# Layer 2 context attention: where the queries' reciprocal roots stand in VectorE's row

## The chip, the core and the metric

The kernel runs on one core of one Trainium2 chip. It is one launch of a program written in Python with a tiling layer: the source emits instructions in an order, and a planner of that layer (it has a cost for each instruction and a list of free buffers) decides the order in which each engine gets them. The engines are PE (TensorE: matrix products and transposes, writes to PSUM), DVE (VectorE), ACT (ScalarE), POOL (GpSimd, no access to PSUM) and SP (issues DMAs). Each runs its own row of instructions in order and waits on semaphores for the others. The metric is the device time of one execution in microseconds, the median of several runs; lower is better.

## What is computed

A decoder of four layers on x of 8 batches x 256 tokens x 256 features, with 77 context rows in each batch. Every layer has an attention, a context attention and a feed-forward part, each followed by a layer norm. The part in question is the context attention of layer 2. Its reference, cut:

```python
q = (x @ q_w.T + q_b).reshape(b, s1, H, hd).transpose(0, 2, 1, 3)      # H = 16, hd = 16
kv = (y @ kv_w.T + kv_b).reshape(b, s2, 2, H, hd).transpose(2, 0, 3, 1, 4)
k, v = (kv[0], kv[1])
q = _layernorm(q, qn_w, qn_b)          # over the 16 numbers of a head, eps 1e-6
k = _layernorm(k, kn_w, kn_b)
q = _apply_rope(q) * scale
attn = jax.nn.softmax(jnp.einsum('bhqd,bhkd->bhqk', q, k), axis=-1)
o = jnp.einsum('bhqk,bhkd->bhqd', attn, v)
return o.transpose(0, 2, 1, 3).reshape(b, s1, c) @ out_w.T + out_b
```

The feed-forward part behind it is a mixture of 14 experts. For every token it needs the two best experts and its place in their lists; this is called the routing here, and the kernel works it out batch by batch inside the context attention, as soon as a batch's layer norm is done.

## The kernel before, in words

A batch is 256 tokens, two tiles of 128. The function of the stage, `l2_xattn`, has one iteration for each of the 8 batches, and works on three of them at once: the weights of batch b, the scores' shift of batch b + 1, and the queries of batch b + 2.

- `queries(b)` projects values and queries on PE (L155). The query weights are centred beforehand, so the layer norm needs only the deviation: ACT squares the projection, DVE sums each head's 16 squares (L1630), and `roots` makes 1/sqrt of 32 numbers per token by integer arithmetic on DVE: scale (L1614), shift (L1615), seed (L1616) and three Newton rounds of three small operations (L1618, L1619, L1620), each of which needs the one before. Then the product of projection and root, 128 x 512, gives `q` (L1732). The projection stays in its PSUM buffer until then.
- `rotated(b, q, v)` does the rotation: two POOL instructions (L1743, in the trace `u`), two on DVE (L1747 and L1748, in the trace `sq`), and a POOL sum (L1749) into `qpad`. All their operands are in SBUF.
- `shift(b, qp, between)` transposes the queries (L293; copied by L141 on DVE and L143 on ACT), computes all scores once (L1763: for each of two tiles four PSUM buffers), and takes the negated maxima over the keys on DVE (L1767, eight of them, `mxp`). Then it calls `between`, and after that transposes the maxima (L1774) and adds them to the queries as one more coordinate (L1775).
- `weights` computes the scores transposed (L1786) and their exponentials on ACT (L1791). `weigh` is what `between` calls: the product with the values (L1805, 32 passes in two halves), copied to SBUF by ACT (L1811, first half) and DVE (L1807, second half). The copy on DVE waits by an explicit dependency for the end of the routing's first part.
- `heads_out` and `project` finish the batch: transposes (L1354), division (L1358, L1363), output projection (L155), residual (L272), layer norm (L249 to L255, with a root by POOL, L183) and transposes of the new x (L235).

Between these, `tick` advances a list of generators by one step each time it is called. For a batch that has its layer norm, `Routing.batch` is in that list. Its first part: product with the router's weights (PE, L155 `rw`), row maximum (DVE L2516), subtraction (L2517), exponential (ACT L2518), sum (L2519), reciprocal (L2520), product (L2521), the eight largest (MAX8, L2524), their indices (L2525), then small operations on them (L2568, L2526, L2570, L2532) up to `rsel`, the one-hot sum of the two chosen experts (L2535), and running counts (L2538). Its second part begins with PE products of `rsel` (L155 `upper`, `onesb`) for the places in the lists, and ends with four indirect DMAs by POOL (L1018).

PSUM has eight buffers of one tag, `ps`; a matrix product into a buffer waits until its former content has been read.

The loop, and where the order comes from:

```python
for b in range(NB):
    e, v = weights(b, q2), ahead[0][1]
    ahead.pop(0)
    if b + 2 < NB:
        begun = queries(b + 2)
    if b + 1 < NB:
        q2 = shift(b + 1, ahead[0][0], lambda: weigh(b, e, v))
    else:
        weigh(b, e, v)
    if b + 2 < NB:
        ahead.append(rotated(b + 2, *begun))
    self.tick()
```

So the root and the product of batch b + 2 are emitted ahead of the score maxima of batch b + 1. The planner interleaves: in the order that it builds, the first round and one operation of the second stand ahead of the first maximum, one Newton operation stands between each two of the next maxima, and the product L1732 between the sixth and the seventh.

## Time and profile before

| what | value |
|---|---|
| median of 3 runs | 3623.32 us (3618.66 to 3629.59) |
| time of the profiled execution | 3594.94 us |
| its span, first to last instruction | 3593.2 us |
| mean granted PE clock in it | 0.896 |
| busy in the span: PE, DVE, ACT, POOL | 86%, 51%, 29%, 26% |
| one batch of the stage, at 2633 us | 27.36 us: PE 22.29, DVE 19.45, ACT 7.22, POOL 11.19 busy |
| the stage in the trace | about 2515 to 2745 us |

How to read the lines below: a line of the timeline gives the start in us, the duration, the engine, the line of the source, the operation, the tile that is written and those that are read, their shapes, and how often; in brackets stands how long the engine was idle before it and what ended that. A line of the waits gives who waited for whom, us in total, how many times, and the longest. A line of the table by stretches gives the stretch, its length, busy time (and instructions) of PE, PE's weight loads, DVE, ACT and POOL, the granted clock of PE, the share of DMA and GB/s.

### The profile page before, as it was taken

How to read it: one execution, taken by the hardware profiler on the slowest of the kernel's cores; microseconds unless marked ns; L12 is line 12 of the kernel's file. 1: busy time of each engine (PE TensorE's matmuls, PEld its weight loads, DVE VectorE, ACT ScalarE, POOL GpSimd, SP SyncE). 2: the span in 40 equal slices, each digit the busy share in tenths (PEclk: the TensorE clock that was granted, in tenths of full speed). 3: DMA queues.
4: the chain of work that ended last, by engine and by line, in shares of the span. 5: the costliest groups of instructions: out<-in, count | busy, mean ns of one | idle time of the engine just before them, and what ended most of it. 6: DMA issues, size and time to landing. Idle time of an engine off the chain costs nothing. (4 is left out here: it accounts for less than half of the span.)

```text
span 3593.2 us, 49384 instructions
## 1 busy us (share of the span) xinstructions
PE 3102.3 (86%) x19146; PEld 2184.7 (61%) x19146; DVE 1834.9 (51%) x4823; ACT 1043.6 (29%) x2343; POOL 928.1 (26%) x1398
## 2 busy tenths in 40 slices
PE   4777589979997998998999999898787997778789
PEld 3444257658875665666555777565555785566556
DVE  7888546631116555776211221566675344677652
ACT  4666322212222332332111111344222111343311
POOL 2222513243314101222000000411343444312351
PEclk6777689979998999988999999999777998888889
DMA  9900100035541000001010333200002552000000
GB/s 338 305 2 1 48 7 19 19 108 181 179 144 47 1 25 25 13 14 60 15 36 0 119 124 119 62 1 8 7 19 83 198 196 77 22 1 7 12 5 19
DMA packets 132127, 239.47 MB, mean 67 GB/s; under 512 B 14568, under 2 KB 103920, under 8 KB 124208
## 3 DMA queue, kind: packets, MB, share of 16 engines
q1 hardware_dynamic: 107632, 136.25, 11.3%
q0 software_dynamic: 23104, 98.95, 7.9%
q8 instruction: 154, 2.52, 0.3%
q10 hardware_dynamic: 1152, 1.05, 0.1%
q14 instruction: 85, 0.70, 0.1%
HBM read 156.52 MB, written 79.69 MB: 66 GB/s over the span
## 5 line engine op out<-in xcount | busy, mean ns | idle before, releaser
L155 PE MATMUL ps<-xt,w 128*128 128x256 f32 (+1 forms) x1408 | 452.9, 472 | 3.3 <-issue 2.9
L155 PE MATMUL ps<-w,hT 128*128 128x256 f32 (+1 forms) x1792 | 397.4, 379 | 0.0
L155 PEld LDWEIGHTS ps<-w,hT 128*128 128x128 f32 (+1 forms) x1792 | 329.9, 186 | 56.5 <-issue 6.0
L155 PE MATMUL ps<-gT,w 128*128 128x256 f32 (+1 forms) x1472 | 357.4, 401 | 5.7 <-ACT gT L143 3.0
L155 PEld LDWEIGHTS ps<-xt,w 128*128 128x128 f32 x1408 | 268.7, 198 | 149.4 <-issue 125.0
L155 PEld LDWEIGHTS ps<-gT,w 128*128 128x128 f32 x1472 | 276.5, 191 | 76.8 <-ACT gT L143 3.9
L155 PE MATMUL ps<-w,oT 128*128 128x256 f32 x768 | 181.9, 390 | 3.3 <-DVE mv L251 1.8
L267 POOL TENSOR_TENSOR xb<-x,rows 128x256 f32<-128x256 f32 x96 | 71.6, 752 | 401.7 <-DVE res L272 393.7
L155 PEld LDWEIGHTS ps<-w,oT 128*128 128x128 f32 x768 | 146.4, 194 | 38.5 <-issue 14.1
L235 PE MATMUL ps<-ident,x 128*128 128x128 f32 x320 | 62.0, 307 | 79.5 <-DVE x L255 59.4
L1115 ACT ACTIVATE hT<-ps,more 128x256 f32<-128x256 f32 x152 | 71.9, 474 | 196.1 <-PE ps L155 196.1
L255 DVE TENSOR_SCALAR x<-res,mv,rs 128x256 f32<-128x256 f32 x128 | 57.4, 449 | 126.9 <-POOL rs L183 126.9
L1126 DVE COPY y<-ps 128x512 f32<-128x512 f32 x41 | 28.3, 690 | 174.7 <-PE ps L155 174.7
L1184 DVE TENSOR_TENSOR hT<-hT,ps 128x512 f32<-128x512 f32 x56 | 38.5, 688 | 154.2 <-PE ps L155 152.7
L677 ACT ACTIVATE e<-ps,nm 128x128 bf16<-128x128 f32 (+1 forms) x256 | 103.9, 458 | 40.1 <-DVE nm L672 24.1
L932 PE MATMUL ps<-ident,P 128*77 128x128 f32 x512 | 90.0, 303 | 25.5 <-POOL P L923 15.7
L1666 POOL TENSOR_TENSOR kpad<-kpad,rows 128x256 f32<-128x256 f32 (+1 forms) x10 | 7.3, 729 | 404.2 <-DVE hu L1615 316.9
L923 POOL TENSOR_TENSOR P<-P,z 128x1232 f32<-128x1232 f32 x24 | 54.1, 2252 | 219.6 <-DVE z L921 214.3
L183 POOL TENSOR_TENSOR rs<-rs,mhalf 128x1 f32<-128x1 f32 x192 | 106.1, 554 | 14.2
L932 PEld LDWEIGHTS ps<-ident,P 128*77 128x77 f32 x512 | 60.7, 157 | 73.4 <-issue 25.5
L947 PE MATMUL ps<-PT,V 77*64 77x256 f32 x512 | 98.5, 446 | 7.5 <-DVE PT L141 4.9
L1180 ACT ACTIVATE hT<-ps 128x512 f32<-128x512 f32 x56 | 33.4, 597 | 237.5 <-PE ps L155 237.5
(655 smaller groups left out, 6319.2 us busy)
## 6 DMA issues: line engine op xcount, KB each, us to landing
l2x<-zero SPq DMA_DIRECT2D x28, 1024.0 KB, 11.3
l0x<-zero SPq DMA_DIRECT2D x16, 1024.0 KB, 11.3
w<-in_L_ffn_rg SPq DMA_DIRECT2D x8, 1024.0 KB, 7.0
w<-in_L_ffn_ru SPq DMA_DIRECT2D x8, 1024.0 KB, 5.0
w<-in_L_ffn_rd SPq DMA_DIRECT2D x8, 1024.0 KB, 5.7
l2e<-y SPq DMA_DIRECT2D x22, 256.0 KB, 2.3
rows<-in_rows SPq DMA_DIRECT2D x9, 544.0 KB, 3.7
l0e<-y SPq DMA_DIRECT2D x19, 256.0 KB, 2.9
```

The lines of the kernel that those rows point to most:

```text
L155: self.nc.tensor.matmul(out, lhsT, rhs, start=(i == 0), stop=(i == last))
L183: self.nc.gpsimd.tensor_tensor(out, out, self.mhalf[: in_.shape[0], :w], ALU.pow)
L235: self.nc.tensor.transpose(ps[:, k * P : (k + 1) * P], x[:, k * P : (k + 1) * P], self.ident)
L255: nc.vector.tensor_scalar(t, r, mv[:, 0:1], rs, ALU.subtract, ALU.mult)
L267: self.nc.gpsimd.tensor_tensor(t, self.X[i], row, ALU.add)
L677: nc.scalar.activation(e[:, : (t + 1) * P], ps[j][:, i, :], AF.Exp, bias=nm[:, t, h : h + 1], accum_out=z[:, t, h : h + 1],)
L923: eng.tensor_tensor(pr, pr, z.unsqueeze(2).to_broadcast([P, H, SC]), ALU.mult)
L932: nc.tensor.transpose(psv[:, m, t * P : (t + 1) * P], Pt[t][:, 2 * n + m, :], self.ident)
L947: nc.tensor.matmul(po[64 * m : 64 * m + 64, :S], V[:, h * 64 : (h + 1) * 64], ahead[n % 2][:, m, :], start=True, stop=True,)
L1115: nc.scalar.activation(hT[:, f + m, :], ps[:, m * 256 : (m + 1) * 256], func, bias=more[:, f + m : f + m + 1])
L1180: nc.scalar.activation(hT[:, f, :], ps, func, **({"bias": bias(f)} if bias else {}))
L1184: nc.vector.tensor_tensor(hT[:, f, :], hT[:, f, :], ps, ALU.mult)
```

## The change

`deviations` now ends with the sum of squares and leaves the root to its callers; for the keys (`l2_keys`) the two calls follow each other as before. `queries` becomes a generator: its first step emits the projections, squares and sums, its second step the root and the product. The first two batches run both steps at once. In the loop the first step is taken where `queries` stood, and the second in `between`, that is, after all eight maxima and after the call of `tick` that emits the routing's first part, and ahead of `weigh`. `rotated` is emitted where it was.

```diff
@@ deviations
         nc.vector.tensor_reduce(v, sq, AX.X, ALU.add)
-        return self.roots(v, 1.0 / 16, 1e-6)
+        return v
@@ l2_keys
-                r = self.deviations(pool, kh, H)
+                r = self.roots(self.deviations(pool, kh, H), 1.0 / 16, 1e-6)
@@ queries
                 r = self.deviations(w2, ps.rearrange("p (n d) -> p n d", d=16), 32)
+                yield
+                r = self.roots(r, 1.0 / 16, 1e-6)
                 q = self.t(w2, [P, 2, H, 16], "q")
                 ...
-                return q, v
+                self.begun = q, v
@@ l2_xattn
+            def all_of(gen):
+                for _ in gen:
+                    pass
+                return self.begun
+
+            def between(b, e, v, gen):
+                all_of(gen)
+                weigh(b, e, v)
+
-            ahead = [rotated(0, *queries(0))]
-            begun = queries(1)
+            ahead = [rotated(0, *all_of(queries(0)))]
+            begun = all_of(queries(1))
...
-                if b + 2 < NB:
-                    begun = queries(b + 2)
+                gen = queries(b + 2) if b + 2 < NB else iter(())
+                next(gen, None)
                 if b + 1 < NB:
-                    q2 = shift(b + 1, ahead[0][0], lambda: weigh(b, e, v))
+                    q2 = shift(b + 1, ahead[0][0], lambda: between(b, e, v, gen))
...
-                    ahead.append(rotated(b + 2, *begun))
+                    ahead.append(rotated(b + 2, *self.begun))
```

Lines behind L1730 have other numbers in the changed kernel: the product L1732 is L1734 there, L1747 to L1749 are L1749 to L1751, the maxima L1767 are L1769, L1805 is L1807, and those of the routing are 11 higher (L2519 is L2530, `rsel` L2546).

## The prediction

> **What bounds the kernel now.** The page first: PE is busy 86% of the span, DVE 51%, but that is an average over twelve layers. The change touches only the L2 context attention, which stands in the trace from about 2515 to 2745 us. So I went to the waits inside the five batches that carry routing work (2570 to 2700 us; total us, times, longest):

> ```profile
> PE ps L155 <- DVE rsel L2535: 12.2, 5, 2.8
> ...
> PE ps L1763 <- DVE mxp L1767: 5.8, 5, 1.2
> ...
> DVE rm L2519 <- ACT rs L2518: 0.6, 1, 0.6
> ```

> TensorE stands still once in every batch for `rsel`, the routing's one-hot sum, which is the last of a long row of DVE instructions. All that PE does after it in the batch (routing ranks, transposes of the maxima, L1786 scores) is queued behind it, so the DVE row from the score maxima to `rsel` sets the batch. The timeline of the batch at 2605 us shows that row (start, us, engine, line):

> ```profile
> 2605.13 0.19 DVE L1618 TENSOR_TENSOR hu<-hy 128x32 f32<-128x32 f32 x1
> 2605.24 0.47 DVE L1767 TENSOR_REDUCE mxp<-ps 128x4 f32<-128x308 f32 x1
> ...
> 2607.95 3.64 PE L1805 MATMUL ps<-e,vp 77*32 77x256 f32 x32
> 2608.06 0.68 DVE L1732 TENSOR_TENSOR q<-ps,hy 128x512 f32<-128x512 f32 x1
> ...
> 2608.82 2.13 POOL L1743 TENSOR_TENSOR u<-q,other 128x256 f32<-128x256 f32 x2 [6.96 <-DVE q L1732]
> ...
> 2609.52 0.70 DVE L1747 TENSOR_TENSOR sq<-q,own 128x512 f32<-128x512 f32 x1
> ...
> 2609.94 0.59 ACT L1811 COPY oT<-ps 128x512 f32<-128x512 f32 x1 [7.92 <-PE ps L1805]
> ...
> 2610.14 0.17 DVE L2517 TENSOR_TENSOR rs<-ps,rm 128x28 f32<-128x28 f32 x1
> 2610.26 1.24 DVE L1748 TENSOR_TENSOR sq<-sq,more 128x512 f32<-128x512 f32 x1
> 2610.43 0.23 ACT L2518 ACTIVATE rs<-rs 128x28 f32<-128x28 f32 x1
> ...
> 2611.42 0.17 DVE L2519 TENSOR_REDUCE rm<-rs 128x2 f32<-128x28 f32 x1
> ...
> 2611.67 1.26 POOL L1749 TENSOR_TENSOR qpad<-sq,u 128x512 f32<-128x512 f32 x1 [0.72 <-PE ps L1805]
> 2611.82 1.15 DVE L2521 TENSOR_TENSOR rs<-rs,rm 128x28 f32<-128x28 f32 x1
> 2613.01 0.25 DVE L2524 MAX8 rv<-rs 128x8 f32<-128x14 f32 x2
> ...
> 2614.16 0.19 DVE L2535 TENSOR_TENSOR rsel<-rhot 128x28 bf16<-128x28 f32 x1
> ...
> 2614.40 0.19 PE L155 MATMUL ps<-rsel,upper 128*128 128x14 bf16 x1 [2.81 <-DVE rsel L2535]
> ```

> Three things are to be seen. DVE has no gap in this row. ACT's exponential (L2518) stands in ACT's queue behind the copy L1811, which waits for half of PE's L1805. And two DVE instructions are longer than their kind: L2521 takes 1.15 us here and 0.19 where POOL is idle (2718.93 us); L1748 takes 1.24 and 0.64 alone (2563.31 us). Each ends just after a POOL instruction does: DVE operations with two operands in SBUF wait for POOL's. The batches at 2633, 2660 and 2687 us repeat this to 0.2 us; batch lengths are 27.42, 27.36 and 27.35 us.

> **What the built order says.** No instruction is added or removed on any engine; PE, ACT, POOL and SP keep their order, no DMA moves, no PE instruction waits for the later query product. Only DVE's order changes, in six batches (queries 2 to 7). The planner does not put all the root behind the maxima: scale, shift, seed and the first Newton round stay ahead. After that: 4 maxima, round two (3 operations), 4 maxima, L2516, one operation, L2517, two operations, **L2519, product L1732**, L2520, L1747, L2521, L1748, MAX8. Before, round two and three and the product stood between the maxima.

> **Cost, in us after 2605.13** (before → after).
> - A copy now stands ahead of the scale instead of behind it, where it hid the scale's result: the copy's step 0.33 (2603.70 to 2604.03) plus scale to shift 0.21 (2555.13 to 2555.34), against 0.42: +0.12. The first maximum no longer waits for an operation of round two (a dependent step is 0.225): 0.11 → 0.01. PE's last scores wait for that maximum, so PE gains 0.10.
> - Maxima follow each other in 0.41 (eight in 3.34 at 2712.33: (3.34 − 0.47)/7). Round two, uncovered, is at 1.65, 1.87, 2.10; the second four start at 2.20, the last at 3.43 (before 3.91). L2516: 4.30 → 3.84; L2517: 5.01 → 4.05. Root operations end by 4.56.
> - **The new wait.** DVE now stands at L2519. The exponential was at 5.30 because of ACT's copy and PE's L1805; PE's 0.10 makes it 5.20, and its result is read 0.26 later (2584.25 to 2584.51): L2519 6.29 → 5.46, after 0.9 us of idle DVE. Queued behind it: the product and all of the rotation.
> - Product 2.93 → 5.55, ends 6.23. L1747 can start at 6.27, POOL's pair L1743 at 6.31 (0.08 behind the product, as now). Before, POOL's pair began at 3.69, beside maxima that read PSUM; now it meets L1747, L2521 and L1748, all with two SBUF operands. L1747 holds POOL to 6.88 (0.61, as at 2609.52), the first of the pair (1.65/2 = 0.82 alone at 2560.14) goes to 7.70, L2521 to 7.74, the second to 8.54, L1748 ends 0.55 later at 9.09 and MAX8 starts at 9.01 (before 7.88).
> - POOL's L1749 then runs from 9.17 to 10.43 (1.26). DVE's L2568, two operands, is due 0.51 after MAX8, at 9.52, and ends at 10.47 instead; `rsel` follows 0.50 later: **9.03 → 10.97, +1.94**.

> That POOL and DVE take turns is shown by the one place where the product is directly followed by L1747 today, in the prologue:

> ```profile
> 2529.30 0.69 DVE L1732 TENSOR_TENSOR q<-ps,hy 128x512 f32<-128x512 f32 x1
> 2530.10 1.36 DVE L1747 TENSOR_TENSOR sq<-q,own 128x512 f32<-128x512 f32 x1
> ```

> L1747 is held for 0.67 by POOL's first, started 0.03 before it.

> The batch at 2577 has its exponential late already (L2519 at 7.11 after its first operation, idle 0.56). There 7.11 − 0.10 + 5.51 = 12.52 against 9.22: +3.3. The batch at 2556 has no routing; DVE runs without a gap there too, and two root operations and the product now stand ahead of the copy L1807 (2560.75 → about 2561.33): +0.6. Sum: 0.6 + 3.3 + 4 × 1.94 = **+11.7**. Nothing hides it: PE's wait grows by the same amount.

> **The clock** is unpriced by this. PE's granted clock falls in each batch and comes back after `rsel` (span, busy us, clock, DMA):

> ```profile
> 2607.60:2617.80 10.20, 7.38 (x54) 5.04 (x54) 9.59 (x37) 0.71 (x2) 3.54 (x4) 0.50 0.00 1
> 2617.80:2634.90 17.10, 14.74 (x145) 10.55 (x144) 9.74 (x34) 6.51 (x16) 7.65 (x12) 1.00 0.09 32
> ```

> L1805 takes 3.64 us in the first and 1.93 at full clock (2558.13). Warm and cold lengths are near 5 × and 3 × 3.41; a later `rsel` can add one more such step at half clock, in which PE loses at most half: 0 to 1.7 a batch, 0 to 8.5 over five. The nearest row is the batch at 2577: `rsel` 0.19 later than in the next one, the batch 0.31 longer, so 0.12 over. I take 0.3 a batch, 1.5 in all. The other way, a clock that falls later would let L1805 end its first half up to 0.86 earlier (half of 3.64 − 1.93), and L2519 with it: −4.3 over five batches.

> [...]

> [...]

> 11.7 + 1.5 = **+13**. Against the profiled execution (span 3593.2, time 3594.94 us) that is 3608; the median of the runs shown is 28 above that, 0.8% of the whole, which on 13 us is 0.1, so the difference is added as it is: 3623.3 + 13 = **3636**.

> **Rivals.**
> - **Not slower: the port does not decide.** If POOL's three reads fall beside MAX8, the searches and the casts (one operand each), the row is L1747 6.27, L2521 6.88, L1748 6.98, MAX8 7.55, `rsel` 8.70: −0.33 in four batches, +1.0 in the fifth, +0.6 in the first, together +0.3, so 3624; with a later clock fall −4, 3619. It decides once `rsel` comes before 9.0. For it: the second maxima end 0.48 earlier. Against: the 1.15, 1.24 and 1.36 us rows.
> - **DVE keeps the port between its own operations**: MAX8 at 7.55, POOL's pair collides later with L2568 and L2532; `rsel` 9.6 to 10.7, sum +5 to +10, say 3630. Against: L1748 lost to the waiting POOL in five batches.
> - **The clock adds a full step in most batches**: +20, 3643.
> - **The move does nothing**, because the planner restores the old order: excluded by the built order for DVE; what is left is a delay of `rsel` absorbed by later waits: 3623.

> **How the numbers follow.** Two measurements of this kernel tell apart about 0.3%, 10.9 us. Chances: forecast 0.60, DVE keeps the port 0.12, not slower 0.17, clock step 0.08, absorbed 0.03. Of the forecast 0.50 lies above 3634.2; with the clock case 0.58 slower. Within: 0.10 of the forecast, 0.12, 0.12 of the third and 0.03, so 0.37. Faster, 0.05, needs the port free and the clock late at once. The range, 3622 to 3648, runs from the port that does not decide to 11.7 + 8.5 and 4 more.

> **What would show it.** Right: DVE idle near 0.9 before L2519 in four batches; L2521, L1748 and L2568 stretched to 0.8 to 1.3; PE's wait for `rsel` 4 to 5 us in place of 2.81; batches of 29 to 30 us. Wrong: L2519 without a wait; L2568 at 0.14; batch lengths at 27.3; or waits grown and the later layers starting no later.

## The result, and the profile after

The changed kernel takes **3635.03 us** (median of 9 runs, 3633.0 to 3639.56) against 3623.32 (9 runs): ratio 1.0032, 95% interval 1.0024 to 1.0040, so 8.7 to 14.5 us slower. Measured once more on another chip (run a0 below), where the kernel before takes 3596.4, it is 1.0048 (1.0035 to 1.0061). The kernel before takes some 26 us less on the later chips than in the first measurement, so only ratios to the kernel before on the same chip are compared below.

The two profiled executions cannot be subtracted as wholes: the spans differ by 38.8 us (3632.0 against 3593.2), of which 8.1 are there already ahead of the six batches and 9.6 arise behind them in one stall of PE (from 2813.6 us on; the trace names no releaser for it, and the second profile of the changed kernel does not have it). The profiles of the unchanged before (b0) and after (a0) on the later chips differ by 12.4 us in span, and by 13.2 between the starts of the first and the last of the six batches. The effect is in those batches and goes on in the sixth, whose `rsel` comes another 3.05 us later: counted from the first start, the layer's last `rsel` is 16.0 us later in a0 than in b0, and 17.5 later in after than in before.

The waits of the five batches with routing work, in the changed kernel (us total, times, longest):

```profile
PE ps L155 <- DVE rsel L2546: 22.1, 5, 4.4
...
DVE rm L2530 <- ACT rs L2529: 8.8, 5, 1.9
...
PE ps L1765 <- DVE mxp L1769: 5.2, 5, 1.1
```

PE's wait for `rsel` has gone from 12.2 to 22.1 us, and a wait that was there once (0.6, at the exponential) is there five times, 8.8. PE's wait for the maxima shrank by 0.6 in all. The timeline of a steady batch, changed kernel:

```profile
2613.14 0.68 DVE L1630 TENSOR_REDUCE qv<-sq 128x32 f32<-128x512 f32 x1
...
2616.39 1.98 PE L1765 MATMUL ps<-l2kT,qT 32*128 32x77 f32 x26 [1.15 <-DVE mxp L1769]
...
2620.12 3.64 PE L1807 MATMUL ps<-e,vp 77*32 77x256 f32 x32
2620.23 0.19 DVE L2527 TENSOR_REDUCE rm<-ps 128x2 f32<-128x28 f32 x1 [0.59 <-PE ps L155]
...
2622.13 0.59 ACT L1813 COPY oT<-ps 128x512 f32<-128x512 f32 x1 [9.38 <-PE ps L1807]
...
2622.61 0.23 ACT L2529 ACTIVATE rs<-rs 128x28 f32<-128x28 f32 x1
...
2622.87 0.18 DVE L2530 TENSOR_REDUCE rm<-rs 128x2 f32<-128x28 f32 x1 [1.91 <-ACT rs L2529]
2622.97 0.68 DVE L1734 TENSOR_TENSOR q<-ps,hy 128x512 f32<-128x512 f32 x1
...
2623.69 0.69 DVE L1749 TENSOR_TENSOR sq<-q,own 128x512 f32<-128x512 f32 x1
2623.73 2.68 POOL L1745 TENSOR_TENSOR u<-q,other 128x256 f32<-128x256 f32 x2 [11.15 <-DVE rm L2531]
2624.30 0.82 DVE L2532 TENSOR_TENSOR rs<-rs,rm 128x28 f32<-128x28 f32 x1
2625.04 0.68 DVE L1750 TENSOR_TENSOR sq<-sq,more 128x512 f32<-128x512 f32 x1
...
2626.49 1.26 POOL L1751 TENSOR_TENSOR qpad<-sq,u 128x512 f32<-128x512 f32 x1
2626.54 1.35 DVE L2543 TENSOR_TENSOR rhot<-io,rix 128x28 f32<-128x28 f32 x2
...
2627.93 0.19 DVE L2546 TENSOR_TENSOR rsel<-rhot 128x28 bf16<-128x28 f32 x1
...
2628.17 0.19 PE L155 MATMUL ps<-rsel,upper 128*128 128x14 bf16 x1 [4.41 <-DVE rsel L2546]
```

Read it from the bracket of 1.91: DVE has done everything that it may and waits for ACT's exponential, which ran right behind the copy L1813, which waited for PE's L1807. Product and rotation are queued behind that. Then POOL's pair takes 2.68 us (1.65 alone), L2532 0.82 (0.19 alone), and the first `rhot` comparison 1.25 of the 1.35: three operations that lost a turn. And PE's scores L1765 and its weighing L1807 run at half clock here; in the kernel before, the same scores and the router's products behind them still ran at full clock:

```profile
2605.76 1.11 PE L1763 MATMUL ps<-l2kT,qT 32*128 32x77 f32 x26 [1.16 <-DVE mxp L1767]
2606.81 1.21 PE L155 MATMUL ps<-rw,xt 128*128 128x14 f32 x8
```

They take 1.98 and 1.89 us now. The clock of this and the next stretch (span, busy PE, PE loads, DVE, ACT, POOL, clock, DMA):

```profile
2615.70:2632.70 17.00, 11.90 (x94) 8.90 (x98) 13.36 (x51) 0.71 (x2) 5.02 (x4) 0.50 0.01 1
2632.70:2646.40 13.70, 12.33 (x106) 8.43 (x102) 6.12 (x19) 6.65 (x16) 6.73 (x11) 1.00 0.12 39
```

Before, a batch had 10.2 us at half clock and 17.1 at full; now 17.1 at half and 13.7 at full. In the batch shown, the fall comes 2.5 us after the batch's reduce (L1630) in place of 5.2; in the next three it comes 2.1, 1.6 and 1.2 us after it, in place of 5.0, 5.0 and 4.9.

### The profile page after: what moved, and what is told of

It reads as the page before. It is cut to its first block, busy times and chain, and to the rows that moved or that the text cites. A ratio compares the mean times of both kernels' runs of the same rounds, so it can differ in the third digit from the quotient of the medians.

```text
span 3632.0 us, 49373 instructions
## 1 busy us (share of the span) xinstructions
PE 3121.7 (86%) x19135; PEld 2199.0 (61%) x19146; DVE 1833.5 (50%) x4823; ACT 1044.6 (29%) x2343; POOL 929.4 (26%) x1398
## 5 line engine op out<-in xcount | busy, mean ns | idle before, releaser
L155 PE MATMUL ps<-xt,w 128*128 128x256 f32 (+1 forms) x1408 | 453.1, 472 | 3.3 <-issue 2.9
L155 PE MATMUL ps<-w,hT 128*128 128x256 f32 (+1 forms) x1792 | 397.4, 379 | 0.0
L155 PEld LDWEIGHTS ps<-w,hT 128*128 128x128 f32 (+1 forms) x1792 | 329.9, 186 | 56.5 <-issue 6.0
L155 PE MATMUL ps<-gT,w 128*128 128x256 f32 (+1 forms) x1472 | 357.9, 401 | 6.8 <-ACT gT L143 3.0
L155 PEld LDWEIGHTS ps<-xt,w 128*128 128x128 f32 x1408 | 268.8, 198 | 149.8 <-issue 125.1
L155 PEld LDWEIGHTS ps<-gT,w 128*128 128x128 f32 x1472 | 276.6, 191 | 78.6 <-ACT hT L1115 4.5
L155 PE MATMUL ps<-w,oT 128*128 128x256 f32 x768 | 184.2, 394 | 3.3 <-DVE mv L251 1.9
L155 PEld LDWEIGHTS ps<-w,oT 128*128 128x128 f32 x768 | 147.9, 196 | 39.1 <-issue 15.3
```

The lines of the kernel that those rows point to most:

```text
L155: self.nc.tensor.matmul(out, lhsT, rhs, start=(i == 0), stop=(i == last))
```

## Theory, rivals and the runs

**Theory 1**, the prediction's: the exponential behind ACT's copy (a new wait), POOL and DVE taking turns (one waits while the other runs; below, it has then "lost a turn"), and half-clock steps that follow from a later `rsel`. **Theory 2**: the clock's phase alone makes the batch long, whatever DVE does. **Theory 3**: the whole-kernel difference comes from elsewhere, or what is won before `rsel` is lost later.

All runs in one table. `rsel` is counted from the batch's reduce; lengths are from reduce to reduce, for the batches behind the one at 2577; "five" is from the first to the last of the six starts (batches of queries 2 to 7), and the half-clock time in these is given in steps of 3.413 us, of which it is a whole number in every run.

| run | rsel, us | lengths of three batches | five | steps at half clock | ratio to before (95%) |
|---|---|---|---|---|---|
| before / b0 | 11.73 | 27.42 27.36 27.35 | 130.6 | 13 | 1.0001 (0.9991 to 1.0010) |
| after | 14.79 | 31.13 31.21 31.18 | 144.6 | 19 | 1.0032 (1.0024 to 1.0040) |
| a0 | 14.78 | 31.00 30.87 30.80 | 143.8 | 19 | 1.0048 (1.0035 to 1.0061) |
| a_exp | 12.48 13.24 12.12 | 29.15 28.73 27.47 | 134.2 | 14 | 1.0018 (1.0009 to 1.0027) |
| a_rot | 12.67 12.67 11.48 | 29.39 28.86 27.68 | 134.7 | 15 | 1.0012 (1.0003 to 1.0020) |
| a_rot_exp | 10.76 10.77 10.76 | 27.22 27.26 27.28 | 129.4 | 15 | 0.9991 (0.9982 to 1.0000) |
| a_nopool | 13.02 11.36 13.02 | 28.80 27.18 29.75 | 135.7 | 17 | 0.9997 (0.9988 to 1.0006) |
| a_fill | 13.91 13.10 13.60 | 29.74 27.86 28.35 | 135.3 | 10 | 1.0026 (1.0016 to 1.0035) |
| b_nopool | 11.62 10.22 11.63 | 27.45 26.61 27.67 | 129.6 | 15 | 0.9987 (0.9978 to 0.9996) |
| b_exp | 11.93 11.72 11.72 | 27.49 27.29 27.31 | 130.5 | 14 | 0.9994 (0.9985 to 1.0003) |
| b_rot | 11.61 10.64 11.62 | 27.82 26.84 27.80 | 131.1 | 15 | 0.9998 (0.9989 to 1.0007) |
| b_rot_exp | 9.69 9.69 9.49 | 26.60 26.60 26.01 | 126.8 | 13 | 0.9982 (0.9973 to 0.9991) |
| b_fill | 11.93 11.92 11.93 | 27.18 27.24 27.29 | 129.6 | 12 | 0.9991 (0.9982 to 1.0000) |

An a_ run edits the changed kernel, a b_ run the kernel before. Line numbers behind an edit move by up to five.

### b0 and a0: both kernels once more

No edit.

> The kernel before, unchanged, once more: a profile of its own on the chip that runs the next three kernels, and a measure of what two sets of runs of one kernel differ by. All theories: 1.000 of the kernel before within 0.2% (3616 to 3631 us), batches of 27.35 to 27.45 us with PE's wait for rsel 2.6 to 2.8. If the profile of before that is shown was an unusual execution, its span differs from 3593 by up to 30 us while the batches stay the same length.

> The kernel after, unchanged, on the chip that runs the next three kernels. All theories: 1.0024 to 1.0040 of the kernel before, batches of 31.1 to 31.3 us, rsel 14.8 us after the reduce of the batch's queries.

b0 repeats the batches of before within 0.05 us and its time within the interval: the shown profile of before was no odd one in the stage. a0 repeats the changed row to 0.03 us. Its batches are 0.1 to 0.4 us shorter than those of after, just below the length expected, and its median is a little above the range expected (1.0048, interval 1.0035 to 1.0061; this interval and that of after meet only at 1.0035 to 1.0040).

### a_exp and b_exp: the exponential ahead of ACT's copy

```diff
-                        nc.scalar.copy(o[:, 2 * gp : 2 * gp + 2, :], ps)
+                        cp = nc.scalar.copy(o[:, 2 * gp : 2 * gp + 2, :], ps)
+                        if routed is not None:
+                            self.after(cp.ins, [self.expd.ins])
...
-            nc.scalar.activation(s, s, AF.Exp)
+            g.expd = nc.scalar.activation(s, s, AF.Exp)
```

> The kernel after, with ACT's exponential of the routing put ahead of the copy of the weighed values in ACT's queue; DVE's order is untouched. Theory 1 (new wait behind that exponential, turns between POOL and DVE, and half-clock steps that follow from the later rsel): DVE's idle time before L2530's sum falls from 1.91 to below 0.6, the sum starts near 7.3 us after the reduce of the batch's queries in place of 9.73, rsel near 12.4 in place of 14.79, the batches 27.5 to 29.5 us in place of 31.2, the kernel 7 to 17 us below after: 3618 to 3628. Theory 2 (the clock's phase alone: the batch is long because half speed begins earlier, whatever DVE does): batches stay at 30.5 or more and the kernel within 3 us of 3635. Theory 3 (the whole-kernel difference comes from elsewhere): the batches get shorter and the kernel stays at 3635.

A batch of a_exp; the copy now stands behind the exponential:

```profile
2608.63 0.23 ACT L2531 ACTIVATE rs<-rs 128x28 f32<-128x28 f32 x1 [7.19 <-DVE rs L2530]
...
2608.89 0.18 DVE L2532 TENSOR_REDUCE rm<-rs 128x2 f32<-128x28 f32 x1
...
2609.52 0.58 ACT L1813 COPY oT<-ps 128x512 f32<-128x512 f32 x1 [0.67 <-PE ps L1807]
...
2611.06 1.37 DVE L1750 TENSOR_TENSOR sq<-sq,more 128x512 f32<-128x512 f32 x1
```

The sum has no bracket any more: DVE does not wait. It starts 7.05 after the reduce in place of 9.73 (7.79 in one batch), the five lengths fall from 143.8 to 134.2, and the ratio to 1.0018. That is theory 1, a little short of its gain: the expected 3618 to 3628 are ratios up to 1.0013. (By the medians the gain over a0 is clear of noise; against the first measurement of after the intervals still overlap, from 1.0024 to 1.0027.) In three batches L1750 lost a turn (1.37), which the expectation, built on the changed kernel's order of turns, did not have. Theory 2 asked for 30.5 a batch and theory 3 for an unmoved kernel; both are out as the whole story.

> The kernel before with ACT's routing exponential ahead of the copy, DVE's order unchanged. Theory 1: in four of five batches DVE has no idle time before the sum, so nothing is won there; only the batch at 2577 (idle 0.56) gains, 0.5 to 2 us; the kernel 0.9990 to 1.0003 of before. Rival (the exponential's place is worth the same with and without the change, some 6 us): 0.9980 to 0.9986.

In the kernel before, the same edit moves `rsel` by 0.2 us at most and five lengths by 0.1: 0.9994, no difference that this interval shows. So in four of the five batches this wait is one that the change makes; only the batch at 2577 had it before (0.56 us).

### a_nopool and b_nopool: the rotation without POOL

```diff
-                for u in range(2):
-                    nc.gpsimd.tensor_tensor(
-                        u2[:, :, :, u::2], q[:, :, :, 1 - u :: 2], over(other[:, :, :, u]), ALU.mult
-                    )
...
-                nc.vector.tensor_tensor(u1, u1, over(flat(more)), ALU.add)
-                nc.gpsimd.tensor_tensor(qp, u1, u2, ALU.add)
+                nc.vector.tensor_tensor(qp, u1, over(flat(more)), ALU.add)
```

> The kernel after without POOL in the rotation: the sine half of the rotation is left out, and DVE's own addition writes the queries. Theory 1: from L2530's sum to rsel 3.2 to 3.5 us in place of 5.06 (L2532 at 0.19, the first rhot at 0.15 to 0.3), while DVE's idle time before the sum stays near 1.9; rsel 1.6 to 1.9 earlier, batches 28 to 29.5 us, the kernel 7 to 15 us below after: 3620 to 3628. Theory 2 (clock's phase alone): rsel earlier, batches still above 30.5, the kernel within 3 us of 3635. A rival within theory 1, that the turns are small beside the wait: under 0.8 us of the 5.06 goes.

> The kernel before without POOL in the rotation: the sine half of the rotation is left out, and DVE's own addition writes the queries. Theory 1: the sum stays where ACT's exponential sets it (9.0 after the reduce of the batch's queries), L2521 takes 0.19 in place of 1.15, rsel comes 0.9 to 1.0 earlier, batches 26.0 to 26.6 us, the kernel 3614 to 3620. Between this and the kernel after without POOL 1.6 to 2.8 us a batch remain, 6 to 12 us in all, which are the later product and the wait. If the turns were all that the change costs, nothing would remain; theory 2: 3.8 a batch remain.

These two runs leave out the sine half of the rotation, so they do not compute the same queries; they serve to show what POOL's part costs. Two lines of a_nopool, the routing's product and `rsel`:

```profile
2610.52 0.18 DVE L2527 TENSOR_TENSOR rs<-rs,rm 128x28 f32<-128x28 f32 x1
...
2612.40 0.19 DVE L2541 TENSOR_TENSOR rsel<-rhot 128x28 bf16<-128x28 f32 x1
```

The routing's product takes 0.18 and from the sum (2609.10) to `rsel` there are 3.30 us in place of 5.06: the turns are 1.76 a batch, shown by taking POOL away. In b_nopool the same way is 1.79 in a batch that does not wait, against 2.74: 0.95. Both kernels also win 3.0 us in the prologue (L1747's 1.36 us, of which the prediction showed one, become 0.69). The five lengths now differ by 6.1 in place of 13.2; by medians a_nopool and b_nopool lie 0.0010 apart, with intervals that overlap. So the turns are about half of the change's cost, not all. The expectation for b_nopool that its sum stays at 9.0 was wrong: it was at 9.83 in three batches of five, because PE's clock fell earlier there (1.9 to 2.5 us after the reduce) and the copy came later. POOL's turns are won, and the exponential takes a part back.

### a_rot, b_rot, and both edits together

```diff
-                nc.vector.tensor_tensor(u1, q, over(flat(own)), ALU.mult)
+                ins = nc.vector.tensor_tensor(u1, q, over(flat(own)), ALU.mult)
+                if self.behind is not None:
+                    self.after(ins.ins, [self.behind.ins])
...
                 routed, self.routed = self.routed, None
+                self.behind = routed
```

> The kernel after, with DVE's two instructions of the rotation put behind the routing's first part (behind rsel); the late product and ACT's order stay as they are. Theory 1 (new wait behind ACT's exponential, turns between POOL and DVE, half-clock steps that follow from the later rsel): DVE's idle time of 1.9 before the sum stays, L2532 starts right behind the product at 10.6 and not at 11.15, one or two of DVE's operations still lose a turn to POOL's pair; rsel 11.9 to 12.9 in place of 14.79, batches 28 to 29.7, the kernel 1.0000 to 1.0018 of before. Theory 2 (clock's phase alone): rsel earlier, batches still above 30.5, the kernel above 1.0025.

In a_rot POOL and DVE start 0.02 us apart:

```profile
2616.63 1.63 POOL L1745 TENSOR_TENSOR u<-q,other 128x256 f32<-128x256 f32 x2 [11.15 <-DVE rm L2534]
2616.65 0.85 DVE L2535 TENSOR_TENSOR rs<-rs,rm 128x28 f32<-128x28 f32 x1
```

One turn is still lost (0.85), as theory 1 had it; the rest of the row runs free, from the sum to `rsel` 2.94. The ratio (1.0012, on the chip of a0 with 1.0048) and most of the lengths are where theory 1 put them; two of the four lengths are below its 28 us (27.4 and 27.7), with `rsel` at 11.2 and 11.5.

> The kernel before with DVE's two instructions of the rotation behind rsel, ACT's order unchanged. Theory 1 (the wait behind ACT's exponential, turns between POOL and DVE, half-clock steps that follow): the sum starts as soon as the exponential allows, 8.2 to 8.6 after the reduce of the batch's queries in place of 9.0, with 0.8 to 1.2 idle before it, L2521 at 0.19, rsel 10.0 to 10.4 in place of 11.74, the batches 26.2 to 27.0 us, the kernel 0.9980 to 0.9995 of before; it lies between the kernel before and the one that has the exponential ahead of the copy too (0.9982). Rival: the turns in the kernel before cost nothing (PE's wait ends elsewhere): 1.000.

This one missed. The turns are gone (L2521's twin 0.19), and yet the kernel is at 0.9998 and the batches at 27.8 in three of five. The sum of a batch, with what it waited for:

```profile
2612.94 0.18 DVE L2522 TENSOR_REDUCE rm<-rs 128x2 f32<-128x28 f32 x1 [2.22 <-ACT rs L2521]
```

DVE was ready 1.4 us earlier than before, and waits 2.22 us for the exponential, because in these batches the clock falls 1.6 to 2.2 us after the reduce. The copy, and with it the exponential, then comes at 9.56 in place of 8.0. My expectation had held the clock's place fixed, as the prediction had. By its medians b_rot is where the rival expectation had it, at 1.000: in the kernel before, taking away the turns alone is worth nothing that this run shows.

> The kernel before (product early), with DVE's rotation behind rsel and ACT's routing exponential ahead of the copy: both costs that theory 1 names are taken out of the kernel before. Theory 1: the sum starts 1.3 to 1.6 us earlier than 9.0, L2521 at 0.19 to 0.5, rsel 1.7 to 2.6 us earlier than 11.74, PE's wait for rsel below 1.2, batches 24.5 to 26 us, the kernel 0.9960 to 0.9980 of before (7 to 14 us faster). Theory 3 (whatever is won before rsel is lost later): batches below 26 us and the kernel within 0.1% of before.

> The kernel after with both: the rotation on DVE behind rsel, and the exponential ahead of the copy; the product stays late, behind the sum. Theory 1: what is left of the change is the product itself (0.69) and at most one turn lost to POOL's pair, so the sum starts near 7.05 after the reduce of the batch's queries, L2532 at 7.85 to 8.1, rsel at 9.4 to 10.3, batches 26 to 27.2 us, the kernel 0.9978 to 0.9993 of before, though it has the whole change in it. Rival (the later product costs by itself, through POOL and the queries written later): 1.000 or above.

With both edits the copy no longer stands ahead of the exponential, and the rotation no longer ahead of `rsel`. A batch of b_rot_exp:

```profile
2635.47 0.18 DVE L2524 TENSOR_REDUCE rm<-rs 128x2 f32<-128x28 f32 x1 [0.29 <-ACT rs L2523]
...
2635.88 0.19 DVE L2526 TENSOR_TENSOR rs<-rs,rm 128x28 f32<-128x28 f32 x1
...
2638.22 0.20 PE L155 MATMUL ps<-rsel,upper 128*128 128x14 bf16 x1
```

PE does not wait for `rsel` at all (no bracket). **0.9982 (0.9973 to 0.9991)**: faster than both kernels, and some 6.5 us faster than before. Theory 3 (won before `rsel`, lost later) had asked for a kernel within 0.1% of before; the median lies beyond that, the end of the interval just inside. The gain is a little less than expected: `rsel` is 2.0 us earlier, but the batch only 0.75 to 1.3 shorter (24.5 to 26 us were expected), since PE is now held by its own work ahead of `rsel`, which at half clock ends later than `rsel` comes. a_rot_exp holds the whole change and is at 0.9991, as theory 1 has it: beside the product, one turn is lost (L2537, 0.87). Its `rsel`, 10.0 to 10.8, is a little later than expected. In the trace it is 2.6 us longer over the five lengths than b_rot_exp, so of the 13.2 us that the change costs there 2.6 are left when both kernels have the two edits; by the medians, on two chips, the two are not separated.

### a_fill and b_fill: work for PE in its wait

```diff
                     if gp:
+                    if gp and routed is not None:
+                        fill = self.ps()
+                        for _ in range(32):
+                            nc.tensor.matmul(fill[:, :P], self.identb, self.onesb, start=True, stop=True)
```

(In front of the copy of the second half; 20 in b_fill.)

> The kernel after, with 32 products of 128x128 bf16 that nobody reads added on PE between the second half of the weighing (L1807) and the products with rsel, in the time in which PE waits for rsel (4.41 us). [...] DVE's order is untouched. Theory 1: PE's idle time is what lets the clock stay low: full clock comes back one or two steps of 3.41 us earlier, each step worth up to 1.7 us, batches 28 to 30 us, rsel unchanged or up to 1 us earlier, the kernel 1.0000 to 1.0025 of before. If the clock's steps do not depend on that wait: batches 31.2 and the kernel 1.0024 to 1.0040, as after. If the added work itself lowers the clock: longer.

> The kernel before with 20 products of 128x128 bf16 that nobody reads added on PE in its wait for rsel; at the 0.11 us that 32 of them took in the kernel after with them, 2.2 us of the 2.6 to 2.8. Nothing else moves. If PE's idle time keeps the clock low: full clock returns one step of 3.41 us earlier in some batches, these 1 to 1.7 us shorter, the kernel 0.9985 to 0.9998 of before. If the clock's steps do not depend on it: 27.3 a batch and 1.000. If the added products delay the ones with rsel: above 1.000 by at most 0.0005.

PE in a batch of a_fill:

```profile
2619.23 3.59 PE L1811 MATMUL ps<-onesb,identb 128*128 128x128 bf16 x32
2623.72 0.19 PE L155 MATMUL ps<-rsel,upper 128*128 128x14 bf16 x1 [0.89 <-DVE rsel L2550]
```

Useless work shortens the stage: 19 steps at half clock become 10, the five lengths 143.8 become 135.3, with DVE's order untouched. From the sum to `rsel` the row is still 5.07; what moved is the sum (8.0 to 9.4 in place of 9.73, since PE's weighing begins earlier) and PE's work behind `rsel`. So PE's idle time is what keeps the clock low here, and in the trace the clock carries up to 8.4 of the 13.2 us. By the medians the gain over a0 on the same chip is 1.0048 to 1.0026, at the edge of the two intervals, and a little above the 1.0025 that was expected at most. b_fill shows the same sign (13 steps to 12, 1.0 us over five lengths, 0.9991 with 1.0000 at the edge); in it the added products delay the ones with `rsel` by 0.7 to 0.8.

## Point by point: where the prediction held and where it did not

The kernel, forecast at +13 us, is +11.7 (8.7 to 14.5), and +17 (13 to 22) in the second measurement; the five lengths in the traces, +13 to +14. That the sum came out is in part luck. Two of its terms were wrong by more than a microsecond a batch, in opposite directions. And the five lengths hold only three of the four steady batches that it adds up: for them it gives 9.7, or 11 with its clock term, and by the layer's last `rsel` 16.0 to 17.5 us were lost in the traces where it has 13. The direction and the places of the cost were right; a steady batch was sized too small (`rsel` +1.94 predicted, +3.05 measured, and 3.5 to 3.8 us in the batch's length). In the prediction's own frame (us after the row's start, 2615.85 in the changed kernel):

| step | before | predicted | measured |
|---|---|---|---|
| first maximum | 0.11 | 0.01 | 0.01 |
| row maximum (L2516) | 4.30 | 3.84 | 4.38 |
| subtraction (L2517) | 5.01 | 4.05 | 4.60 |
| exponential (L2518) | 5.30 | 5.20 | 6.76 |
| sum (L2519) | 6.29 | 5.46 | 7.02 |
| product (L1732) | 2.93 | 5.55 | 7.12 |
| MAX8 | 7.88 | 9.01 | 9.79 |
| rsel | 9.03 | 10.97 | 12.08 |

- **The row before the wait: held up to the maxima.** First maximum 0.01, the second four at 2.16 (2.20 predicted); round two's dependent steps took 0.21 and 0.23 us uncovered, as by the rows. L2516 then waits 0.59 for PE's `rw` products, which at half clock take 1.89 in place of 1.21; the prediction had no wait there.
- **The new wait: right in kind, half its size.** DVE idles 1.91, not 0.9, and the sum comes 0.73 later than before instead of 0.83 earlier. The step that failed is "PE's 0.10 makes it 5.20": it kept PE's weighing at its old place. It began 1.45 us later, after scores at half clock. a_exp shows that the copy is the cause; b_exp that the wait is new in the steady batches.
- **The batch at 2577: +3.3 predicted; `rsel` came 1.37 later and the batch was 2.05 longer.** The same error the other way. There the clock fell 2.2 us after the reduce before, and falls 5.0 after it now, so the exponential that was late there came at 7.97 in place of 9.56.
- **The turns: right, and the order wrong.** From sum to `rsel` 5.51 predicted, 5.06 measured, 2.74 before. L1749 and L2532 behaved as said. L1750 did not lose its turn to POOL's second (0.68; POOL waited, 1.38), and POOL's L1751 then held the first `rhot` (1.25), not L2568. In a_exp L1750 wins in two batches and loses in three, and `rsel` differs by 0.36 for that. Which DVE operations give way is read from the traces: beside POOL, L2532 with its two operands in SBUF takes 0.82 in place of 0.19, while MAX8, with one, takes 0.16 beside POOL as without it (both in the changed kernel), and L2517, which reads `ps`, takes 0.17 beside POOL's pair in the kernel before (none of POOL's 1398 instructions there names a `ps` buffer). Who goes first is the one that started first in a_rot's pair (POOL 0.02 earlier, DVE 0.85 in place of 0.19) and with L1749 (0.04 ahead of POOL, 0.69 long, 0.68 alone). With L1750 it is not: in all ten batches with routing work of after and a_exp the trace has POOL's second start 0.004 to 0.007 us ahead of it, and DVE won in seven of them.
- **What `rsel`'s +3.05 is made of**, by b_nopool and a_nopool: 0.73 the later sum, 1.51 product and rotation behind the sum (1.79 to 3.30 without POOL), 0.81 more turns (0.95 to 1.76).
- **The clock: the mis-sized term.** 0.3 a batch was taken, with 1.7 as its end. Measured: two more steps of 3.41 us at half clock and one fewer at full in each steady batch. Its cost has no single number, since an early fall also delays the sum; a_fill gives 8.4 us of 13.2 back by filling PE's wait, a_exp 9.6 by the exponential's place, a_rot 9.1 by the rotation's place. These sum to twice the effect: each of them also takes the clock's steps away.
- **The first batch**: +0.6 predicted, +0.56 measured (21.32 against 20.76).
- **The rivals.** "The port does not decide" and "DVE keeps the port" are refuted by the stretched rows (L2532 0.82, `rhot` 1.25) and a_nopool (3.30 from sum to `rsel` in place of 5.06); no run shows a port, only the turns. "The clock adds a full step" is half true: the steps are there, and more than one, but the kernel's +11.7 stays below its +20 in the first measurement (the second's interval takes 20 in). "Absorbed" is refuted.

## What to carry to other kernels

Before moving work behind a barrier on one engine, look at the engine that feeds the barrier: here the barrier was an exponential queued behind a copy, and everything placed behind it inherited that copy's lateness (DVE waited 1.91 us). Where a trace shows two engines taking turns, count the turns by order of start (0.04 us was enough for L1749), expect a near tie to go either way (L1750, less than 0.01 apart), and keep the long pair away from the short operations on the path: put behind `rsel` the rotation no longer delays it (from the sum to `rsel` 2.94 us in a_rot in place of 5.06), and together with the exponential ahead of the copy that gave the fastest kernel of this study, while alone (b_rot) it gave nothing. And do not hold the clock's place fixed in such a sum: a later result that leaves PE idle also costs half-clock time, here up to 8.4 of 13.2 us.

## What was not expected of the hardware

- **The batches fall into step with the clock.** 8 × 3.413 is 27.31 and 9 × 3.413 is 30.72. Batches of before (27.42, 27.36, 27.35), b_exp (27.29, 27.31; its other one, 27.49, is 0.18 off), b_fill (27.18 to 27.29) and a_rot_exp (27.22 to 27.28) lie within 0.13 of the first, though PE gets `rsel` from 11.0 to 12.8 us after the reduce in them; a0 (31.00, 30.87, 30.80) closes in on the second. That a batch is held to a whole number of steps would explain why single removals gave back 9 of 13 us and b_rot nothing. It is argued from these lengths, not shown: no run moved the steps alone. The shown profile of the changed kernel (31.13 to 31.21) does not close in on the second value, and a_exp, a_rot, a_fill, b_rot and b_rot_exp have batches off both.
- **Work that nobody reads can pay**: 32 products in PE's wait made the stage 8.4 us shorter in the trace (by the medians, a gain at the edge of noise).
- **Two operations that start less than 0.01 us apart** (L1750 and POOL's second) go in either order, in the same kernel, from batch to batch; POOL's starts in the trace may be too rough to tell which came first.
